# Attention over four head pairs in a row in place of two, with the queries and keys of four pairs kept, in a three-layer kernel on one core

## The chip, the core and the metric

The kernel runs on one NeuronCore of a Trainium2 chip. The metric is the device time of one execution in microseconds (us), the median of several. The engines are TensorE (PE, with its weight loads PEld), VectorE (DVE), ScalarE (ACT), GpSimd (POOL) and SyncE (SP, which here issues DMAs). SBUF is the on-chip memory of 128 partitions, PSUM the accumulators that PE writes. PE, DVE, ACT and POOL each work through their own instructions in program order and wait for each other by semaphores.

## The reference

The input x is 8 batches of 512 rows of 256 numbers, float32. Three residual layers and a fourth that has the third's form:

```
x = x + linear(layernorm(x))     # Q,K,V = xn @ W.T; Q,K normalised by row; Q * mean_n(K * V)
x = x + ffn(layernorm(x))        # r = sigmoid(xr @ W_r.T); k = relu(xk @ W_k.T)**2; r * (k @ W_v.T)
x = x + attention(layernorm(x))  # 16 heads of 64: softmax(q k.T / 8) v, over axis 2; output product l_w, l_b
x = x + ffn(layernorm(x))        # the same weights; xr, xk mix each row with the row before it
```

The softmax of the attention runs over the queries: `scores = einsum('bhqp,bhkp->bhqk', q, k) / sqrt(64)` and `softmax(scores, axis=2)`.

## The kernel before

All weights stay in SBUF. The program is written out without loops on the chip, in an order that a planner in the Python code (`class Order`) chooses while the kernel is built. It knows five engines T (PE), A (ACT), V (DVE), G (POOL), S (SP), an estimated cost for each step, the time at which each engine and each of its five PSUM places comes free, and a due period for every piece of work. `CHOICES` holds three numbers for each period: an offset of the share of other work, a slack, and a seed that reorders pieces that are equally ready.

**Attention.** The 8 batches have 16 heads each, so 8 head pairs a batch and 64 pairs in all, numbered g. For a pair, `scores(g, c)` computes a chunk of 128 keys against 512 queries for both heads in four 64x64 quarters of PE's array; DVE takes the maximum over the queries (L1100) and ACT the exponentials with their sums (L1111). `scale_v(g, h)` divides the values by the sums (DVE reciprocal L1124, POOL L1128). `context(g, c)` multiplies, again in quarters (L1148), into two PSUM places, which ACT and DVE empty at the pair's end (L1155, L1156). Score tiles take three places of two banks each (`PAIRS = 3`), contexts two of one bank (`BANKS = 2`).

`attend(g)` writes two pairs: the first pair's scores alternate with the contexts of the pair before it, the second's with the first's. The main loop goes over `range(0, G, 2)`. After each two pairs comes a stretch of work on the whole 128x128 array: all that the planner has due by then or finds a share for. The stretches of quarter-array and of whole-array work thus alternate, 32 times over.

**Whole-array work.** `project_pairs(g)` makes queries and keys of pairs g and g+1 in seven block products instead of eight (`seven`, L931 for the products; its sums of blocks on ACT and DVE at L939, L947, L883, L893, L903). Product 2 goes into the PSUM place of product 1, 4 into that of 7, 3 into that of 5, and each waits until the place's first content has been read. The results stand in `qk` tiles of the pool `heads`, two buffers. `values_fast` does the same for the values, `keys` for the keys of an ffn (L591), `project_out` the output product (tile `y`, L440) of four pairs, whose `ctx` tiles come from the pool `cpool` with eight buffers.

`linear(b, h)`, `queries`, `mean`, `front` and `ffn` (called f0 to f7 after the linear layer, g0 to g7 after the attention) take half a batch each. From batch 2 on, and for the g ffns but the last, the rows are turned by a DMA transpose (`normed_dma`, SP, between two POOL copies), and both halves' keys are made together by `keys` in seven products from sums of blocks in the tile `sums`. Otherwise `mixed_t` turns them on PE and each half has its own four products for k (L551). Queries, keys and values of a batch need its sums of rows `xts` (`sums_of_rows`, POOL), of which there is one buffer.

Due periods around the change: linear and first ffn of batch b by `due_of`, period 8b-3; `project_pairs(g + 1)` at the end of each period; `values_fast` two or four periods later than its start; `project_out(b, half)` gated to pair 8b+5 or 8b+9.

Of the kernel before, what the change touches and what calls it, by code (L numbers as in the profile page):

```python
# [35 lines left out]


CHOICES = (
    (-4, 2, 90203), (0, 0, 43155), (0, 2, 0), (-2, 2, 77416), (1, 0, 8249), (-2, 1, 93964),
    (0, 0, 0), (-6, 1, 43070), (-2, 0, 51517), (-2, 2, 70093), (-2, 2, 81842), (-1, 2, 0),  # L40
    (1, 0, 13647), (6, 0, 84141), (1, 0, 16079), (4, 1, 90125), (-6, 0, 25271), (0, -1, 56854),
    (-2, 2, 47130), (0, -1, 47424), (0, 1, 8929), (4, 0, 14836), (-6, 0, 64258), (4, 2, 13478),
    (-1, 1, 84848), (2, 2, 74886), (1, 2, 58853), (4, 2, 96692), (6, 0, 82127), (4, 0, 41997),
    (0, 0, 0), (-1, -1, 26368), (6, 0, 83164), (0, 0, 0),
)


# [29 lines left out]
class Order:  # L77
# [5 lines left out]
    def __init__(self):  # L83
        self.free = {"T": 0.0, "A": 0.0, "V": 0.0, "G": 0.0, "S": 0.0}
        self.chains, self.period, self.spent, self.count = [], -1, 0.0, 0
        self.open = -1
        self.marks = {None: 0.0}

        self.banks = [0.0] * (PAIRS + BANKS)
        self.current, self.at = None, 0.0  # L90
# [83 lines left out]

    @property
    def choice(self):
        return CHOICES[min((self.period + 1) // 2, len(CHOICES) - 1)]

    def turn(self, c):

# [47 lines left out]
            self.run(self.first([c for c in a if c not in late] or a))  # L228

    def finish(self):  # L230
        self.period = self.open = 10**6
        while self.chains:
            self.run(self.first(self.able()))
# [3 lines left out]
def kernel(ctx: ExitStack, tc: tile.TileContext, a: dict, out: bass.AP):  # L237
# [18 lines left out]
    two = ctx.enter_context(tc.tile_pool(name="two", bufs=2))  # L256
    small = ctx.enter_context(tc.tile_pool(name="small", bufs=8))
    epool = ctx.enter_context(tc.tile_pool(name="epool", bufs=5))
    cpool = ctx.enter_context(tc.tile_pool(name="cpool", bufs=8))
    heads = ctx.enter_context(tc.tile_pool(name="heads", bufs=2))  # L260
    psum = ctx.enter_context(tc.tile_pool(name="psum", bufs=1, space=bass.MemoryType.PSUM))
    halves_v = ctx.enter_context(tc.tile_pool(name="halves_v", bufs=4))
    ctx.enter_context(tc.manual_schedule())
# [66 lines left out]
    def buffers(own):  # L330

        if own not in sets:
            s = {
                n: one.tile([P, 2, 512], F32, tag=f"{n}{own}", name=f"{n}{own}")
                for n in ("xn", "xr", "xk")
            }

            s["ka"], s["r"] = s["xn"], s["xk"]
            s["sums"] = one.tile([P, 3, HS], F32, tag=f"sums{own}", name=f"sums{own}")
            sets[own] = s  # L340
        return sets[own]

# [19 lines left out]
    def normed(src, name, s, h, ready, early=False):  # L362

        ready = yield "V", 1.2, ready
        mv = small.tile([P, 2, 2], F32, tag="mv", name=f"mv_{name}_{h}")
        for u in range(2):
            st = small.tile([P, 6], F32, tag="st", name=f"st_{name}_{h}_{u}")
            nc.vector.bn_stats(st, src[:, 2 * h + u, :])
            nc.vector.bn_aggr(mv[:, u, :], st)
        xn, rstd = tiles(s["xn"], h), small.tile([P, 2], F32, tag="rstd", name=f"rstd_{name}_{h}")  # L370
        if early:

            ready = yield "G", 1.05, ready
            nc.gpsimd.tensor_scalar(rstd, mv[:, :, 1], LN_EPS, 1.0, ALU.add, ALU.mult)
            nc.gpsimd.tensor_tensor(rstd, rstd, neg_half[:, :2], ALU.pow)
            ready = yield "V", 0.75, ready
            for u in range(2):
                nc.vector.tensor_scalar(
                    xn[:, u, :], src[:, 2 * h + u, :], mv[:, u, 0:1], rstd[:, u : u + 1],
                    ALU.subtract, ALU.mult,  # L380
                )
        else:

            shift = small.tile([P, 2], F32, tag="shift", name=f"shift_{name}_{h}")
            ready = yield "G", 1.4, ready
            nc.gpsimd.tensor_scalar(shift, mv[:, :, 0], -1.0, None, ALU.mult)
            nc.gpsimd.tensor_scalar(rstd, mv[:, :, 1], LN_EPS, 1.0, ALU.add, ALU.mult)
            nc.gpsimd.tensor_tensor(rstd, rstd, neg_half[:, :2], ALU.pow)
            nc.gpsimd.tensor_tensor(shift, shift, rstd, ALU.mult)
            ready = yield "A", 1.0, ready  # L390
            for u in range(2):
                nc.scalar.activation(
                    xn[:, u, :], src[:, 2 * h + u, :], AF.Identity,
                    bias=shift[:, u : u + 1], scale=rstd[:, u : u + 1],
                )
        return ready
# [135 lines left out]
    def ffn(xb, name, s, h, ready, add_on, by_dma, due):  # L532
# [5 lines left out]
        mixed, ready = yield from mix(xb, name, s, h, ready, xr, xk)  # L538
        ka, r = chunks(s["ka"], h), s["r"][:, h, :]
        squared, mark = 0.0, None  # L540
        if by_dma:

            r, mark = s["xr"][:, h, :], (name, "k", h)
            if both((name, "k")):
                order.add(keys(name, s, mixed), *due)
        else:
            done = yield "T", BANK, mixed
            ps = bank(f"k_{name}_{h}")
            for dc in range(KC):
                for kc in range(KC):  # L550
                    nc.tensor.matmul(  # L551
                        ps[:, dc * HS : (dc + 1) * HS], lhsT=fk[:, kc, dc * P : (dc + 1) * P],
                        rhs=xk[:, kc, :], start=(kc == 0), stop=(kc == KC - 1),
                    )
            done = yield "A", 0.6, done
            ps = ps.rearrange("p (k s) -> p k s", k=KC)
            nc.scalar.activation(ka, ps, AF.Relu)
            order.give()
            squared = yield "A", 0.6, done
            nc.scalar.activation(ka, ka, AF.Square)  # L560
# [74 lines left out]
                order.add(linear(b, h), *due_of(b))  # L635

    def due_of(b):
        return (-1 if b == 0 else NP * b - 3), NP

    def adder(b):  # L640

# [9 lines left out]
    def linear(b, h):  # L651
# [16 lines left out]
        for u in range(2):  # L668
# [5 lines left out]
                    start=(kc == 0), stop=(kc == KC - 1),  # L674
                )
            ready = yield "A", 0.8, ready
            vs = two.tile([P, D], F32, tag="av", name=f"av_{b}_{h}_{u}")
            nc.scalar.copy(vs, ps[:, D:])
            nc.scalar.activation(kv[:, u, :], ps[:, :D], AF.Square, accum_out=ss[:, u : u + 1])
            if u == 1:  # L680
                order.add(queries(b, h), *due_of(b))
            ready = yield "V", 0.35, ready
            nc.vector.tensor_mul(kv[:, u, :], ps[:, :D], vs)
            order.give()
        rn = small.tile([P, 2], F32, tag="rn", name=f"rnk_{b}_{h}")
        ready = yield from power(rn, ss, b, h, 0, ready)

# [135 lines left out]
    def sums_of_rows(b, ready):  # L823
# [2 lines left out]
        (b11, b12), (b21, b22) = (  # L826
            (xta[b][:, kc, :HS], xta[b][:, kc, HS:]) for kc in range(KC)
        )
        for i in range(4):
            last = f"qk_{NP * b - 2}" if b else None  # L830
            ready = yield "G", 0.8, ready, -1, last
# [186 lines left out]
    def project_out(b, half):  # L1018
# [1 line left out]
        pairs = range(half * NP // 2, (half + 1) * NP // 2)  # L1020
        lead = 2 * NP * (b == B - 1)
        for tp in range(NT // 2):
            ready = yield "T", 2 * BANK, 0.0, NP * b + 5 + 4 * half
            ps = rows(
                f"y_{b}_{half}_{tp}",
                [ctxt[b, p][:, tp * HS : (tp + 1) * HS] for p in pairs],
                [al[:, p, :] for p in pairs],
            )
            ready = yield "V", 0.62, ready
            xt = half_of(x[b], tp)  # L1030
            nc.vector.tensor_tensor(xt, ps, xt, ALU.add)  # L1031
            order.give()
            if half == 1:
                due = NP * (b + 2) + 1, lead
                order.add(tail(b, tp, ready, due), *due)
        if half == 0:
            order.add(project_out(b, 1), NP * b + 11, lead)
# [120 lines left out]
            ready = order.place("A", 0.5, ready)  # L1158
            order.banks[PAIRS:] = [ready, order.place("V", 0.62, ready)]

    def attend(g):

        for c in range(NT):
            if c == 3:
                order.at_once(scale_v(g, 0))
            scores(g, c)
            if g > 0:
                context(g - 1, c)
            else:
                order.fill(BANK)  # L1170
            exps(g, c)
            order.fill(0.0, 1.0)
        for c in range(NT):
            scores(g + 1, c)
            if c == 1:
                order.at_once(scale_v(g, 1))
            if c > 0:
                context(g, c - 1)
            if c == 3:
                context(g, 3)  # L1180
            exps(g + 1, c)
            order.fill(0.0, 1.0)


    G = B * NP
# [25 lines left out]

    total = B * (2.2 + 6 * BANK + 42 * FAST + 0.43 + 8 * BANK + 2 * FFN) - 4 * BANK - 2 * FFN
    total -= 17 * 1.1 + 7 * 1.1
    total += 2 * FAST - 13 * FAST / 2
    for first in range(0, G, 2):
        g = order.period = first + 1
        order.place("T", CHANGE, 0.0)
        attend(first)
        order.place("T", CHANGE, 0.0)
        order.open = g  # L1220
        for h in range(2):
            order.add(scale_v(g, h), g, 2 * G)
        b, p = divmod(g, NP)
        if p == 5:
            order.add(project_out(b, 0), g + 2)
        if g + 1 < G:
            order.add(project_pairs(g + 1), g, NP)
        if p == 1 and b > 0:
            order.add(values_fast(b, 1), g + 2, NP)
        elif p == 3 and b < B - 1:  # L1230
            order.add(values_fast(b + 1, 0), g + 4, NP)
        share = (total - order.spent) / ((G - first) // 2) + order.choice[0]
        begin = order.spent
        order.until(g, share)
        if g < G - 1:
# [55 lines left out]
```

## Time and profile before

| what | us |
|---|---|
| median of 3 runs | 1146.74 (1146.02 to 1146.79) |
| the profiled execution | 1146.73 |
| its span in the profile | 1144.8 |
| PE busy | 1125.2 |
| DVE busy | 806.0 |
| ACT busy | 679.5 |
| POOL busy | 478.9 |
| first matmul starts at | 6.4 |
| first scores start at | 71.33 |
| last matmul group starts at | 1138.36 |

The page gives busy times, time lines and groups of instructions by line. A line of a time line reads: start, length (both us), engine, line, operation, output and inputs by the program's names, array part in use, shape of the moving operand, and how many instructions were merged. PE takes two passes for each float32 matmul of the program, so the counts of the trace are twice the program's. The ends of matmuls are modelled; their starts are measured. In a row of groups, the numbers behind the bar are busy time and mean length in ns. In a row of windows, the first two numbers bound the stretch, the third is its length, then come the busy times of PE, PEld, DVE, ACT and POOL.

### The profile page before, as it was taken

How to read it: one execution, taken by the hardware profiler on the slowest of the kernel's cores; microseconds unless marked ns; L12 is line 12 of the kernel's file. 1: busy time of each engine (PE TensorE's matmuls, PEld its weight loads, DVE VectorE, ACT ScalarE, POOL GpSimd, SP SyncE). 2: the span in 40 equal slices, each digit the busy share in tenths (PEclk: the TensorE clock that was granted, in tenths of full speed). 3: DMA queues.
4: the chain of work that ended last, by engine and by line, in shares of the span. 5: the costliest groups of instructions: out<-in, count | busy, mean ns of one | idle time of the engine just before them, and what ended most of it. 6: DMA issues, size and time to landing. Idle time of an engine off the chain costs nothing. (4 is left out here: it accounts for less than half of the span.)

```text
span 1144.8 us, 19233 instructions
## 1 busy us (share of the span) xinstructions
PE 1125.2 (98%) x6994; PEld 699.2 (61%) x6994; DVE 806.0 (70%) x1474; ACT 679.5 (59%) x1789; POOL 478.9 (42%) x760
## 2 busy tenths in 40 slices
PE   7999999999999999999999999999999999999998
PEld 4645456656556567666656555766656756665556
DVE  5775777667777767767677777777677777667754
ACT  3546756467663864655655676466574566645653
POOL 4455263224712484217542267343553442523201
PEclk9999999999999999999999999999999999999999
DMA  8000000000001110012100111010200110001001
GB/s 298 1 1 1 1 19 19 10 11 11 19 11 38 29 28 10 10 37 38 20 10 11 37 32 25 10 47 10 29 19 1 22 35 2 19 19 20 1 2 37
DMA packets 61182, 28.64 MB, mean 25 GB/s; under 512 B 51456, under 2 KB 59648, under 8 KB 60576
## 3 DMA queue, kind: packets, MB, share of 16 engines
q1 hardware_dynamic: 59936, 25.70, 9.2%
q8 instruction: 56, 0.92, 0.3%
q10 hardware_dynamic: 864, 1.05, 0.3%
q0 software_dynamic: 288, 0.67, 0.2%
q14 instruction: 38, 0.31, 0.1%
HBM read 10.63 MB, written 4.19 MB: 13 GB/s over the span
## 5 line engine op out<-in xcount | busy, mean ns | idle before, releaser
L1111 ACT ACTIVATE e<-sc,nm 128x512 f32<-128x512 f32 x512 | 347.1, 690 | 123.1 <-DVE nm L1100 123.1
L1100 DVE TENSOR_REDUCE nm<-sc 128x2 f32<-128x1024 f32 x256 | 308.9, 1218 | 69.3 <-PE sc L1095 68.6
L1095 PE MATMUL sc<-qk 64*64 64x512 f32 x2048 | 270.1, 594 | 2.6 <-DVE qk L903 1.7
L1148 PE MATMUL cx<-e,vs 64*64 64x512 f32 x2048 | 269.1, 589 | 0.0
L1128 POOL TENSOR_TENSOR vs<-v,rs 128x256 f32<-128x256 f32 x128 | 79.0, 618 | 381.8 <-DVE rs L1124 353.6
L1148 PEld LDWEIGHTS cx<-e,vs 64*64 64x64 f32 x2048 | 87.2, 133 | 136.9 <-issue 114.5
L1095 PEld LDWEIGHTS sc<-qk 64*64 64x64 f32 x2048 | 76.1, 132 | 138.9 <-issue 86.8
L440 PE MATMUL y<-al,ctx 128*128 128x256 f32 x512 | 116.4, 380 | 0.4 <-ACT prev_f L517 0.4
L440 PEld LDWEIGHTS y<-al,ctx 128*128 128x128 f32 x512 | 96.6, 190 | 17.5 <-ACT e L1111 3.2
L1111 ACT ACTIVATION_READ_ACCUMULATOR e<-sc,nm 128x1 f32 x512 | 105.3, 206 | 0.0
L939 ACT ACTIVATE qk<-m_qk,bias 128x256 f32<-128x256 f32 x124 | 52.2, 475 | 51.7 <-PE m_qk L931 50.1
L1156 DVE TENSOR_TENSOR ctx<-cx,ctx 128x512 f32<-128x512 f32 x64 | 44.3, 692 | 47.3 <-ACT ctx L1155 46.3
L947 DVE SCALAR_TENSOR_TENSOR qk<-m_qk,dbias,qk 128x256 f32<-128x256 f32 x124 | 54.1, 478 | 18.3 <-PE m_qk L931 17.7
L1031 DVE TENSOR_TENSOR x<-y,x 128x512 f32<-128x512 f32 x32 | 22.0, 687 | 35.5 <-PE y L440 35.4
L672 PE MATMUL kv<-wkv,xrl 128*128 128x512 f32 x96 | 44.9, 595 | 0.0
L1155 ACT COPY ctx<-cx 128x512 f32<-128x512 f32 x64 | 37.4, 585 | 10.4 <-PE cx L1148 10.4
L931 PE MATMUL m_qk<-xta,sums_q 128*128 128x256 f32 x124 | 38.0, 388 | 1.0 <-DVE qk L893 0.9
L931 PE MATMUL m_qk<-xta,aq 128*128 128x256 f32 x124 | 38.8, 394 | 0.0
L931 PE MATMUL m_qk<-xts,aq 128*128 128x256 f32 x124 | 37.4, 383 | 0.4 <-DVE qk L883 0.4
L931 PE MATMUL m_qk<-xta,ak 128*128 128x256 f32 x124 | 36.9, 379 | 0.0
L931 PE MATMUL m_qk<-xts,ak 128*128 128x256 f32 x124 | 36.9, 379 | 0.0
L931 PE MATMUL m_qk<-xta,sums_k 128*128 128x256 f32 x124 | 36.9, 379 | 0.0
(303 smaller groups left out, 1941.8 us busy)
## 6 DMA issues: line engine op xcount, KB each, us to landing
out<-x SPq DMA_DIRECT2D x16, 256.0 KB, 2.1
x<-in_x SPq DMA_DIRECT2D x6, 512.0 KB, 4.0
aq<-in_aq SPq DMA_DIRECT2D x1, 1024.0 KB, 8.1
ak<-in_ak SPq DMA_DIRECT2D x1, 1024.0 KB, 10.1
av<-in_av SPq DMA_DIRECT2D x1, 1024.0 KB, 12.1
al<-in_al SPq DMA_DIRECT2D x1, 1024.0 KB, 14.5
x<-in_x ACTq DMA_DIRECT2D x4, 128.0 KB, 4.0
x<-in_x SPq DMA_DIRECT2D x4, 128.0 KB, 4.1
```

The lines of the kernel that those rows point to most:

```text
L440: nc.tensor.matmul(ps[:, u * D : (u + 1) * D], lhsT=lhs[i][:, u * P : (u + 1) * P], rhs=rhs[i], start=(i == 0), stop=(i == n - 1),)
L672: nc.tensor.matmul(ps, lhsT=xt[:, kc, u * P : (u + 1) * P], rhs=wkv[:, kc, :], start=(kc == 0), stop=(kc == KC - 1),)
L931: nc.tensor.matmul(ps[:, w * HS : (w + 1) * HS], lhsT=lhs[w][n - 1], rhs=block_of_rows(b, n), start=start and w == 0, stop=True, skip_grou ...
L939: nc.scalar.activation(dst[:, w, :], ps[:, w, :], AF.Identity, bias=bias[:, w, p : p + 1])
L947: nc.vector.scalar_tensor_tensor(dst[:, w, :], ps[:, w, :], dbias[:, w, p // 2 : p // 2 + 1], part[:, w, :], ALU.add, ALU.add,)
L1095: nc.tensor.matmul(ps[m * HD : (m + 1) * HD, j, :], lhsT=kt[hs, keys], rhs=qt[hs, :], start=True, stop=True,)
L1100: nc.vector.tensor_reduce(nm, ps, AX.X, ALU.max, negate=True)
L1111: nc.scalar.activation(e[:, j, :], ps[:, j, :], AF.Exp, bias=nm[:, j : j + 1], accum_out=sums[g, h][:, c % 2, j : j + 1],)
L1128: nc.gpsimd.tensor_tensor(vs, vh[b, p // 4][:, 2 * h : 2 * h + 2, cols].rearrange("p t (j d) -> p t j d", j=2), rs.unsqueeze(3).to_broadca ...
L1148: nc.tensor.matmul(cx[m][j * HD : (j + 1) * HD, :], lhsT=vsc[g, c // 2][ks, c % 2, j, :], rhs=es[g, c][ks, j, :], start=(c == 0), stop=(c ...
L1155: nc.scalar.copy(ct, cx[0])
L1156: nc.vector.tensor_tensor(ct, cx[1], ct, ALU.add)
```

## The change

- `attend(first, n)` writes n pairs in a row: first two stretches of two pairs, then fifteen of four (`range(4, G, 4)`), so that a batch has two stretches of attention and two of whole-array work.
- `heads` has four buffers for `qk` in place of two; each period projects two times two pairs.
- To make room: `cpool` has seven buffers in place of eight; the first ffn's `sums` tile is gone, so its keys (`name[0] == "f"`) are made in eight plain products, four for each half, as the other path has them; `shift` and `rstd` share a tile; `linear` writes a copy of the values into `xk` in place of a tile of its own.
- `queries(b, h)` are entered after both value products in place of after the first; ACT squares before it copies there.
- `sums_of_rows` waits explicitly for the values of the batch before. Due periods and gates follow the longer period, values are entered after the pairs 3 and 7, and `CHOICES` has 20 rows in place of 34, with other numbers.

```diff
-    cpool = ctx.enter_context(tc.tile_pool(name="cpool", bufs=8))
-    heads = ctx.enter_context(tc.tile_pool(name="heads", bufs=2))
+    cpool = ctx.enter_context(tc.tile_pool(name="cpool", bufs=7))
+    heads = ctx.enter_context(tc.tile_pool(name="heads", bufs=4))
...
-        if by_dma:
+        if by_dma and name[0] == "g":
             r, mark = s["xr"][:, h, :], (name, "k", h)
...
-        return (-1 if b == 0 else NP * b - 3), NP
+        return (-1 if b == 0 else 3 if b == 1 else NP * b - 1), NP
...
-            vs = two.tile([P, D], F32, tag="av", name=f"av_{b}_{h}_{u}")
+            nc.scalar.activation(kv[:, u, :], ps[:, :D], AF.Square, accum_out=ss[:, u : u + 1])
+            vs = tiles(s["xk"], h)[:, u, :]
             nc.scalar.copy(vs, ps[:, D:])
-            nc.scalar.activation(kv[:, u, :], ps[:, :D], AF.Square, accum_out=ss[:, u : u + 1])
-            if u == 1:
-                order.add(queries(b, h), *due_of(b))
...
+        order.add(queries(b, h), *due_of(b))
...
+        if b:
+            yield "G", 0.0, 0.0, -1, f"v_{b - 1}_1"
...
-            ready = yield "T", 2 * BANK, 0.0, NP * b + 5 + 4 * half
+            ready = yield "T", 2 * BANK, 0.0, NP * b + 7 + 4 * half
...
-    def attend(g):
+    def attend(first, n):
         for c in range(NT):
             if c == 3:
-                order.at_once(scale_v(g, 0))
-            scores(g, c)
...
+        for g in range(first + 1, first + n):
+            for c in range(NT):
+                if c == 3 and g < first + n - 1:
+                    order.at_once(scale_v(g, 0))
+                scores(g, c)
+                if c == 1:
+                    order.at_once(scale_v(g - 1, 1))
+                if c > 0:
+                    context(g - 1, c - 1)
+                if c == 3:
+                    context(g - 1, 3)
+                exps(g, c)
+                order.fill()
...
-    for first in range(0, G, 2):
-        g = order.period = first + 1
+    for first, n in [(0, 2), (2, 2)] + [(g, 4) for g in range(4, G, 4)]:
+        g = order.period = first + n - 1
...
-        if g + 1 < G:
-            order.add(project_pairs(g + 1), g, NP)
-        if p == 1 and b > 0:
-            order.add(values_fast(b, 1), g + 2, NP)
-        elif p == 3 and b < B - 1:
-            order.add(values_fast(b + 1, 0), g + 4, NP)
+        for i in range(g + 1, min(g + (3 if g == 1 else 5), G), 2):
+            order.add(project_pairs(i), g, NP)
+        if p == 3 and b > 0:
+            order.add(values_fast(b, 1), g, NP)
+        if p == 7 and b < B - 1:
+            order.add(values_fast(b + 1, 0), g, NP)
```

## The prediction

> **What bounds the kernel now.** I read the page's busy times first, then TensorE's waits, then the time line across two changes of array mode, then the windows of single stretches. The page:
>
> ```profile
> span 1144.8 us, 19233 instructions
> PE 1125.2 (98%) x6994; PEld 699.2 (61%) x6994; DVE 806.0 (70%) x1474; ACT 679.5 (59%) x1789; POOL 478.9 (42%) x760
> PEclk9999999999999999999999999999999999999999
> ```
>
> TensorE (PE) works from 6.4 us until 4.6 us before the end, at the full granted clock. No other engine is above 70%, so the time is PE's work plus the moments in which PE cannot go on. The waits that the profile lists are few:
>
> ```profile
> engine line waited for: us in total, times, longest us
> PE tr_a L406 <- DVE xnFalse L378: 6.4, 1, 6.4
> PE sc L1095 <- DVE qk L903: 1.7, 4, 0.4
> PE m_qk L931 <- DVE qk L893: 0.9, 2, 0.4
> ```
>
> But matmul ends are modelled, so short stops hide in a busy PE. Starts show them. Sixteen passes of y take 3.45 us, so a 128x256 pass steps by 0.216 and a 64x512 pass in a group of eight by 0.107. The time line around one whole-array stretch (lines left out between the third and the fourth):
>
> ```profile
> 303.41 1.90 PE L1148 MATMUL cx<-e,vs 64*64 64x512 f32 x16
> 305.24 0.70 PE L931 MATMUL m_qk<-xta,aq 128*128 128x256 f32 x2
> 305.77 0.59 PE L931 MATMUL m_qk<-xta,ak 128*128 128x256 f32 x2
> ...
> 322.32 0.70 PE L591 MATMUL m_k_g<-xkTrue,sums_f 128*128 128x256 f32 x2
> 322.95 1.09 PE L1095 MATMUL sc<-qk 64*64 64x512 f32 x8
> 323.86 1.04 PE L1148 MATMUL cx<-e,vs 64*64 64x512 f32 x8
> ```
>
> Into the whole array: 16 x 0.107 = 1.72 should end at 305.13, the next starts at 305.24 and its pair takes 0.53 for 0.43, so 0.20 lost. Back into quarters: 0.63 for 0.43 includes a wait's 0.10, and 0.91 for 0.86, so 0.15 lost. A round trip costs 0.35 us. The same bookkeeping over all passes of the run: 4096 x 0.1074 + 2658 x 0.2156 + 176 x 0.431 + 64 x 0.108 = 1095.8 us of work; 37 quarter-array stretches x 0.35 = 13.0; 6.4 before and 4.6 behind; the remaining 25 us are short waits. 8.0 of them lie before the first scores at 71.3, 1.7 in the tail, some 15.3 between, about 12.5 in whole-array stretches and 2.8 in quarter ones. One of the dearest:
>
> ```profile
> 476.09 0.59 PE L591 MATMUL m_k_g<-sumsTrue,sums_f 128*128 128x256 f32 x2
> 477.11 0.70 PE L931 MATMUL m_qk<-xts,aq 128*128 128x256 f32 x2 [0.42 <-DVE qk L883]
> ```
>
> 1.02 for 0.43: 0.59 of waiting and 0.10 in the next pass, where product 7 follows its predecessor's DVE add too closely. A wait just missed costs 0.18 in the same way (0.08 and 0.10).
>
> **Part by part.** The sum is made on the profiled execution: 1146.73 us, of which 1144.8 is the span and 1.9 lies around it; the median of the runs, 1146.74, is the same.
>
> *Round trips.* In the order of the changed program's PE instructions I count 23 quarter-array stretches for 37. They are the 17 of the loop, the last pair's contexts, one break in the first attention (before: 32, 1 and four) and four cuts in three later ones, after a first chunk of scores: there a PSUM place that attention needs is still held by products that must be finished first. 14 x 0.35 = -4.9.
>
> *Keys of the first ffn.* Batches 2 to 7 take eight products per batch for seven. The rows for m_k_f count 24 + 24 + 24 + 12 passes over six batches, 14 a batch, so a product is two passes, 0.43 us. 6 x 0.43 = +2.6, on the path, since PE is. What leaves with it is beside the path: four POOL subtractions of 0.73, five DVE adds of 0.42, two ACT copies of 0.38 a batch. PE's work is thus -2.3.
>
> *The opening.* Before, four whole-array blocks (v, r_f, o_f, k_f of batch 1) stand between the first scores and fill PE while exponentials run; 71.3 to 122 is nearly without waits. In the new order only one (v, 0.86) is left; the others come earlier. I walk it with the trace's durations (scores 0.86, reduction 1.16, pair of exponentials 1.33, three score banks): fourth scores wait for the first exponentials, the eighth start at 11.0 us, the stretch ends at 13.6. Its work is 12 x 0.86 + 0.86 + 0.7 of changes = 11.9, so +1.7. Next stand the 14 matmuls of project_pairs(2) alone, 6.0 us, with nothing between the dependent products: begin on ACT behind the last exponentials at 15.7, add 17.3, join 18.2, product 4, add, product 3 from 19.2 to 20.1, last add, scores at 21.0. That is 7.4 us for 6.0, so +1.4. Together +3.1; bounds 0 (a cover I overlooked) and 5.
>
> *Tail.* The last matmul is now o_g of batch 6, whose sum goes to POOL (1.27) where before o_g of batch 7 went to DVE (0.69): +0.6. Bounds 0 and 2.
>
> *Waits between.* Neither edit names these; the new order decides them. I compared, in both orders, each waiting matmul's cover (PE work since the product that its chain starts from) with the chain (the rows' durations). Beyond the opening 32 waits of before have a chain longer than the cover, 41 of after. The dearest new one: r_g(4,0) stands 1.72 us behind o_f(6,1), while its input needs that bank's DVE release (0.68), four ACT passes (1.9) and a DVE pair (0.88): 1.6 us. Two contexts at starts of stretches (pairs 15 and 47) wait for a last add of keys, 0.6 each; scores of pair 60 for 0.7. By such sums after has some 2 us more. Against that, stretch ends, where a last product, its add and the first scores stand in a row, come half as often. I take +1.3; bounds -6 (the in-between waits shrink by 40%, with the stretches) and +8 (each of the nine further waits at 0.9).
>
> *Longer quarter stretches.* From the third pair on, a pair finds what the second found before: exponentials of the pair ahead end 9.0 us after that pair's start in both places of the trace. The windows of one stretch of two pairs:
>
> ```profile
> core 0: us, PE busy (x) PEld busy (x) DVE busy (x) ACT busy (x) POOL busy (x), PEclk, DMA share, GB/s
> 322.90:336.80 13.90, 13.90 (x129) 4.77 (x128) 11.64 (x15) 10.24 (x29) 1.23 (x2) 1.00 0.00 1
> ```
>
> DVE is at 84% and ACT at 74% while PE is full, and 28 of 32 stretches show no wait at all, so four pairs cost 0. [...]
>
> *At nothing.* The av tile now lies in xk: same ACT and DVE instructions, square before copy. Queries enter one product later, covered by a stretch of 30 us and more. ctx has seven buffers: the first y of a batch must run in the stretch before the eighth ctx, and does. POOL's wait of the row sums for the values of the batch before has only the chain's later steps behind it, at 42% load; SP issues the same transposes and stores, with DMA at 10%. Were that cover gone, a late transpose would show its 3.0 us to landing once a batch.
>
> Sum: -4.9 + 2.6 + 3.1 + 0.6 + 1.3 = +2.7, **1149.4 us**.
>
> **Rivals.** *Waits go with the number of stretches* (faster). If the 15.3 us between the opening and the tail belong to starts and ends of stretches, halving these takes 7.6: -4.9 + 2.6 + 3.1 + 0.6 - 7.6 = -6.2, 1140.5; it beats no change from 3.2 us of saved waits (21% of them). For it: the chains of two pairs cover each other's adds. Against: about half of the 32 tight waits stand at such an end, but the count of 41 for the new order has its fewer ends in it already. *Opening covered* (about the same): without 3.1 and with waits unchanged, -1.7, 1145.0; without the latter's third, within 0.2%. *Banks* (much slower): two product chains hold up to six of five banks, next to ffn and values; in the order, product 7 of both pairs often waits for the other's add. If each of the 15 stretches pays one wait like the 0.69 at 477.11 on top, +10, 1159. Against: DVE has 12.6 us less to do.
>
> **How the numbers follow.** About 0.2% (2.3 us) is what a measurement here can tell from no change. Forecast case, 1147.5 to 1152: 0.45. Fewer waits, 1139 to 1144.5: 0.25. Covered opening, 1144 to 1147.5: 0.15. Banks, 1152 to 1160: 0.15. Of the forecast case 0.10 lies below 1149.0, of the covered one 0.03 below 1144.4. Faster 0.28, same 0.22, slower 0.50. The range leaves out the ends of the first and last rivals: 1142 to 1156, of which 1147.5 to 1152 is the likeliest case's own.
>
> **What would show it.** The 84 passes of m_k_f gone and 96 of k_f in their place, 2.6 us more; the quarter stretches 27.5 us long without waits inside; a stop of over 1 us before r_g of batch 4's first half; a first stretch of 13 to 14 us, followed by 7 us of m_qk alone. If starts of PE lose less than 20 us beyond the round trips, I am wrong towards the fast side; if the 27.5 us stretches show a wait at each new pair, my reading of the steady state is wrong; if DVE waits before product 7 add up to 5 us or more, the banks have it.

## The result, and the profile after

The changed kernel takes **1171.81 us** (median of 4 runs, 1169.46 to 1172.51), the kernel before, beside it on the same chip, 1146.62 (1146.02 to 1146.79). The ratio is 1.0214, 95% interval [1.0202, 1.0227]: 25 us slower. The forecast said 1149.4 with a range up to 1156; the direction was right, the size was not.

The page of the changed kernel, the lines that answer to those of before (the profiled execution took 1172.51 us):

```profile
span 1170.7 us, 19410 instructions
PE 1132.7 (97%) x7006; PEld 709.3 (61%) x7006; DVE 790.1 (67%) x1444; ACT 677.7 (58%) x1777; POOL 462.9 (40%) x736
PEclk9999999999999999999999999999998999999999
```

DVE and POOL have less to do than before, as the plain keys promise, and PE is still the engine that sets the time. PE's granted clock, 9 in every slice before, now shows one 8. What PE waits for, from the view of waits (us in total, times, longest):

```profile
PE r_g L441 <- DVE xrTrue L524: 3.9, 3, 1.9
PE sc L1097 <- DVE qk L905: 2.9, 3, 1.6
PE kv L673 <- POOL xrl L429: 2.7, 1, 2.7
...
PE k_f L552 <- issue: 1.2, 1, 1.2
PE m_k_g L592 <- DVE xnTrue L895: 1.2, 1, 1.2
PE m_qk L933 <- DVE qk L885: 1.1, 1, 1.1
```

Before, no wait after the first matmul was listed at over 0.9 us; here there are stops of 1.9 and 2.7 us. The same bookkeeping over the starts of PE's passes as in the prediction gives this table. "Waits" is the span less the first matmul's start, the work, 0.35 us for each quarter-array stretch, and the tail; it holds the opening's waits and the passes at half clock too. All columns behind the median are of the profiled execution. The last six rows are of experiments told below.

| kernel | median, us | span | work of PE | stretches: round trips | waits |
|---|---|---|---|---|---|
| before | 1146.62 | 1144.8 | 1095.8 | 37: 13.0 | 25.1 |
| after | 1171.81 | 1170.7 | 1098.4 | 23: 8.0 | 52.7 |
| before, other table (e3) | 1151.32 | 1149.5 | 1095.8 | 37: 13.0 | 29.8 |
| after, other table (e4) | 1165.32 | 1165.0 | 1098.4 | 22: 7.7 | 47.4 |
| after, SP counted, other table (e9) | 1150.09 | 1148.6 | 1098.4 | 23: 8.0 | 30.5 |
| the same with eight places (e10) | 1140.13 | 1138.1 | 1098.4 | 22: 7.7 | 20.8 |
| before, both, other table (e14) | 1134.97 | 1132.6 | 1095.8 | 37: 13.0 | 12.9 |
| after, both, other table (e15) | 1136.70 | 1134.9 | 1098.4 | 24: 8.4 | 17.4 |

So the whole miss is in one column: waits went from 25.1 to 52.7 us, +27.6, where the forecast had +1.3 and +3.1 for the opening. Most of it sits in few places. Three whole-array stretches, in the view of windows (bounds, length, busy PE, PEld, DVE, ACT, POOL, clock):

```profile
285.60:334.10 48.50, 45.48 (x192) 34.61 (x188) 33.40 (x73) 22.09 (x59) 32.71 (x51) 1.00 0.11 21
706.60:761.20 54.60, 51.59 (x219) 40.75 (x215) 31.73 (x72) 25.78 (x66) 32.25 (x51) 0.97 0.12 25
845.60:910.80 65.20, 59.50 (x244) 46.23 (x240) 38.79 (x93) 33.73 (x82) 45.02 (x69) 0.95 0.13 25
```

By their passes they hold 43.55, 49.16 and 54.76 us of work: 4.9, 5.4 and 10.4 us are lost, 20.8 of the 52.7 (1.6 and 2.7 of it, in the last two, at half clock, told at the end). No engine is full in them: DVE is at 58 to 69%, ACT at 46 to 52%, POOL at 59 to 69%. And yet PE waits for each of them in turn. The time line ahead of the dearest stop, cut to POOL, SP's queue and the waiting product:

```profile
714.33 1.17 POOL L420 COPY xrl<-xnl 128x512 uint16<-128x512 uint16 x2
715.70 1.31 SPq L425 DMA_TRANSPOSE xnl<-xrl  x1
717.74 1.34 POOL L429 COPY xta<-xkFalse 128x1024 uint16<-128x1024 uint16 x1 [0.60 <-DMA xkFalse<-xrFalse]
719.01 1.27 POOL L784 TENSOR_TENSOR x<-x,lb 128x512 f32<-128x512 f32 x1
720.22 1.33 POOL L429 COPY xrl<-xnl 128x1024 uint16<-128x1024 uint16 x1
721.60 0.70 PE L673 MATMUL kv<-wkv,xrl 128*128 128x512 f32 x1 [2.65 <-POOL xrl L429]
```

Transposes land 3.1 us after issue (median of this run), so `xrl`'s data were there at about 718.8. The copy that turns them into an input for PE starts at 720.22, because the addition of an output bias, for which nobody waits, stands in front of it in POOL's list. One of the three stops before `r_g`, cut to PE, ACT and DVE:

```profile
871.07 1.89 PE L441 MATMUL o_f<-fv,xnFalse 128*128 128x256 f32 x8
871.27 0.60 ACT L565 ACTIVATE xkFalse<-r_f 128x512 f32<-128x512 f32 x1 [1.23 <-PE r_f L441]
871.76 0.98 ACT L518 ACTIVATE prev_g<-xrTrue,omu 128x255 f32<-128x255 f32 x2
...
873.07 0.69 DVE L570 SCALAR_TENSOR_TENSOR xkFalse<-xkFalse,o_f 128x512 f32<-128x512 f32 x1 [1.23 <-PE o_f L441]
873.88 0.87 DVE L524 SCALAR_TENSOR_TENSOR xrTrue<-xrTrue,mu,prev_g 128x256 f32<-128x256 f32 x2
874.50 1.97 PE L441 MATMUL r_g<-fr,xrTrue 128*128 128x256 f32 x8 [1.55 <-DVE xrTrue L524]
```

`r_g` is a product of the last ffn of batch 4, `r_f` and `o_f` belong to the first ffn of batch 6: no data pass between them. But ACT's shifted rows for `r_g` stand behind ACT's tanh of `r_f`, which waits for PE; and DVE's mix for `r_g` stands behind DVE's product with `o_f`, which waits for PE as well. Two chains that have nothing to do with each other are tied together by the order of the lists, and PE, whose own list is in order too, waits at each knot.

### The profile page after: what moved, and what is told of

Read it like the earlier page. It is cut to its first block, busy times and chain, and to the rows that moved or that the text cites. A ratio compares the mean times of both kernels' runs of the same rounds, so it can differ in the third digit from the quotient of the medians.

```text
span 1170.7 us, 19410 instructions
## 1 busy us (share of the span) xinstructions
PE 1132.7 (97%) x7006; PEld 709.3 (61%) x7006; DVE 790.1 (67%) x1444; ACT 677.7 (58%) x1777; POOL 462.9 (40%) x736
## 5 line engine op out<-in xcount | busy, mean ns | idle before, releaser
L1097 PE MATMUL sc<-qk 64*64 64x512 f32 x2048 | 267.2, 592 | 4.3 <-DVE qk L905 2.9
L1150 PEld LDWEIGHTS cx<-e,vs 64*64 64x64 f32 x2048 | 90.4, 133 | 137.8 <-issue 107.8
```

Of the source, the lines that this page charges most:

```text
L1097: nc.tensor.matmul(ps[m * HD : (m + 1) * HD, j, :], lhsT=kt[hs, keys], rhs=qt[hs, :], start=True, stop=True,)
L1150: nc.tensor.matmul(cx[m][j * HD : (j + 1) * HD, :], lhsT=vsc[g, c // 2][ks, c % 2, j, :], rhs=es[g, c][ks, j, :], start=(c == 0), stop=(c ...
```

## The experiments

Theories, from the expectations: **structure** (two long whole-array stretches a batch leave chains uncovered in whatever order), **order** (the loss lies in the particular order), **chain** (data arrive late along norm, sum and transpose), **queues** (in e5 to e7: ACT, DVE and POOL are too full in the long stretches; from e8 on: a step stands behind steps of other chains in its engine's list), **banks** (too few PSUM places), **eight products**.

### Two kernels with flat tables (e1, e2)

```diff
-CHOICES = (
...
-)
+CHOICES = (
+    (0, 0, 0),
+)
```

> The kernel before, with its table of choices flat: every row (0, 0, 0), so that neither shares, slack nor tie-breaks are bent; the same work in another order. It says how much of 1146.7 us the table carries. Theory 'structure' (two long whole-array stretches a batch leave the chain of steps of a batch uncovered, in whatever order): the table is worth little, 1150 to 1165. Theory 'order' (the loss of 25 us lies in the particular order that the changed kernel's table gives, not in the length of the stretches): a table carries more than the whole difference, over 1172 here.

> The changed kernel with the table flat in the same way. Structure: 25 us above the flat kernel before, give or take 5, since the stretches are what costs. Order: also tens of us above 1172; its distance to the flat kernel before may be anything between -20 and +40, because each is one draw of an order. A distance near +25 alone would not tell the two apart; the next two runs do.

Measured, one run each: 1223.59 and 1235.18. The table carries 77 us in the kernel before and 63 in the changed one, two and a half to three times the difference that was to be explained. "Structure" had expected 1150 to 1165 for the first. The distance of 11.6 is one draw of each and tells nothing alone.

### Tables drawn alike (e3, e4)

The rows of `CHOICES` alone are others.

> The kernel before with a table drawn anew: rows chosen one after the other, with a fixed number of tries each, for the least idle TensorE that the kernel's own planner foresees. It is the yardstick for the next run, same procedure. Both theories: 1146 to 1156, as the table of before is a good one already.

> The changed kernel with a table drawn anew in the same way; everything else as in the changed kernel (four pairs a period, eight products, buffers). Structure: 1163 to 1172, within 9 us of the changed kernel, and some 20 us above the run before it. Order: 1146 to 1158, that is 14 to 26 us below the changed kernel, and within 8 us of the run before it; the stops of over 1 us in whole-array stretches, some 20 us in the changed kernel, fall to less than 8.

Measured: 1151.32 (ratio to before 1.0039 [1.0025, 1.0053]) and 1165.32 (1.0162 [1.0135, 1.0189]). Both theories had the first run. The second is 6.5 us below the changed kernel and 14.0 above its yardstick: inside what "structure" had (1163 to 1172, within 9 us of the changed kernel), though it had put some 20 us above the yardstick, and outside what "order" had (1146 to 1158). So after this pair "structure" stood the better. But the trace of the second shows where its worst stop comes from, and it is a queue that nobody had counted:

```profile
660.78 0.38 SPq L1054 DMA_DIRECT2D out<-x  x1
662.96 0.38 SPq L273 DMA_DIRECT2D x<-in_x  x1
663.44 1.24 SPq L425 DMA_TRANSPOSE xkTrue<-xrTrue  x1
668.47 1.32 POOL L429 COPY xrTrue<-xkTrue 128x1024 uint16<-128x1024 uint16 x1 [6.43 <-DMA xkTrue<-xrTrue]
669.82 0.19 ACT L512 COPY edge_g<-xrTrue 128x2 f32<-128x2 f32 x1 [6.05 <-POOL xrTrue L429]
669.92 0.98 ACT L518 ACTIVATE prev_f<-xrFalse,omu 128x255 f32<-128x255 f32 x2
670.83 0.82 ACT L941 ACTIVATE qk<-m_qk,bias 128x256 f32<-128x256 f32 x2
671.71 0.70 PE L933 MATMUL m_qk<-xta,sums_q 128*128 128x256 f32 x2 [4.27 <-ACT qk L941]
```

The store of a finished batch (L1054) and the load of a new one into the same tile (L273, which waits for the store) stand on SP ahead of a transpose; the transpose, 3.9 us after the POOL copies that feed it ended at 659.52, then takes 4.9 us behind the 512 KB of the load in place of 3.1. POOL waits for it, ACT's two-number copy of an edge waits for POOL, and behind that copy stand the activations that PE needs. The planner gave the store and the load no time on SP.

### The data cut, the order kept (e5, e6)

```diff
     def normed(src, name, s, h, ready, early=False):
+        if name[0] == "g" or name[1:] not in ("0", "1"):
+            src = al
         ready = yield "V", 1.2, ready
```

> The changed kernel, every instruction in the same order, but the norms of batches 2 to 7 and of all last ffns read the rows of a weight that is long there, in place of the batch's rows. So no norm waits any more for a sum that TensorE's products feed; the steps behind a norm, the queues, the PSUM places and the work stay as they are (the output is that of other rows). Theory 'chain' (products wait for the steps that run from one product over a sum, a norm, POOL's copies, a transposing DMA to the next product, and with two stretches a batch too little else stands between): the waits outside the opening fall by more than half, 1140 to 1153. Theory 'queues' (ACT, DVE and POOL, in order, are too full in the long whole-array stretches, whoever feeds them): 1162 to 1172. Theory 'banks' (too few PSUM places): 1162 to 1172 as well, with the waits behind adds of products left.

> The same cut in the kernel before, order kept. Chain: it has little to gain, as an attention stretch of 14 us lies over each link: 1138 to 1146, a gain of less than a third of that of the changed kernel. Queues and banks: 1144 to 1148, no gain.

Measured: 1172.13 (1.0214 [1.0197, 1.0231]) and 1146.71 (0.9995 [0.9986, 1.0004]). Nothing moves. The stops are at the same products with the same lengths (2.77, 1.71 and 2.38 us where the changed kernel has 2.82, 1.71 and 2.10, by the starts of passes). "Chain" in the form in which I held it is refuted: that a norm waits for its rows costs nothing in these orders. What a norm's later steps wait for, their data or their turn, this run does not tell.

### One kind of POOL step taken out (e7)

```diff
-        nc.gpsimd.tensor_tensor(xh, xh, lb.to_broadcast([P, 2, D]), ALU.add)
```

> The changed kernel without the 16 POOL additions of the output bias (1.32 us each, left out of the result), all else in the same order. In the changed kernel's trace one of them stands between two POOL copies of which the second is what TensorE waits for longest (2.65 us at 721.6). Chain: this stop falls by 1.3 us, others hardly, 1166 to 1171. Queues: POOL has 21 us less to do, of which a good part is in the whole-array stretches: 1155 to 1165. Banks: no change, 1169 to 1173.

Measured: 1168.58 (1.0183 [1.0168, 1.0198]), 3.2 us less. The stop at `kv` goes from 2.82 to 1.51 us, that is by the 1.3 us of the addition in front; the three stops from 871 on stay (1.71, 2.12, 2.36). The half-clock passes behind the `kv` stop (told at the end) are gone too (mean granted clock 0.999 for 0.995), and a stop of 1.4 us before the next `r_g` has come in. The time is in the range of "chain", which e5 had already refuted; "queues" in its form of too full engines had 1155 to 1165 and fails. Of some 20 us of POOL work (16 additions of 1.27) leaving it out gained 3.2, part of it clock: here the position of a step counted, not the load.

### Shifted rows in SBUF (e8)

```diff
-            ps = bank(f"prev_{name}_{h}_{i}").rearrange("p (k s) -> p k s", k=KC)
+            order.take()
+            ps = two.tile([P, 512], F32, tag="prev", name=f"prev_{name}_{h}_{i}")
+            ps = ps.rearrange("p (k s) -> p k s", k=KC)
...
```

> The changed kernel, order kept; the shifted rows of a time mix ('prev', two ACT passes and two DVE steps each) lie in SBUF instead of one of PSUM's five places (their two buffers take the room of the value bias, for which another weight's row is read). Theory 'banks' (products and prevs queue for five places): the waits of ACT for a place, and TensorE's behind them (the stops of 1.5 and 1.9 us before r_g at 874 and 878), fall: 1150 to 1164. Theory 'queues' (each engine works its list in order, so that a step stands behind a step of another chain that itself waits for TensorE): within 4 us of the changed kernel, 1168 to 1173.

Measured: 1178.03 (1.0270 [1.0253, 1.0287]), 6 us slower: inconclusive for the question, since the edit changed something else. DVE's mixing steps, here (L525) and in the changed kernel (L524), duration ns min/median/max:

```profile
L525 DVE SCALAR_TENSOR_TENSOR xkTrue<-xrTrue,mu,prev_g x28: 472/486/1487, 298.9 to 1135.3; 128x256 f32<-128x256 f32 x28
L525 DVE SCALAR_TENSOR_TENSOR xrTrue<-xrTrue,mu,prev_g x28: 472/798/1504, 305.4 to 1139.2; 128x256 f32<-128x256 f32 x28
```

```profile
L524 DVE SCALAR_TENSOR_TENSOR xkTrue<-xrTrue,mu,prev_g x28: 472/478/482, 298.7 to 1129.3; 128x256 f32<-128x256 f32 x28
L524 DVE SCALAR_TENSOR_TENSOR xrTrue<-xrTrue,mu,prev_g x28: 473/478/481, 305.0 to 1132.7; 128x256 f32<-128x256 f32 x28
```

With one operand in PSUM all these steps take 472 to 482 ns; with both in SBUF up to three times that.

### The order, with SP counted (e9), and eight places (e10)

```diff
+        stored = yield "S", 0.4, order.marks["g", b, h]
         nc.sync.dma_start(out=rows_out[:, ts, :], in_=x[b][:, ts, :])
         if both(f"g{b}") and b + 4 < B:
+            yield "S", 2.4, stored
             load_x(b + 4)
...
+        if b == 0:
+            ready = max(ready, order.marks.get("sums_q", 0.0), order.marks.get("sums_k", 0.0))
         order.marks["xts", b] = ready
```

> The changed kernel with another order: its planner also counts the store of a finished batch and the load of a new one on SyncE's queue (they were free for it, and in the run with the table drawn anew two transposes behind such a load landed after 6.0 and 4.9 us in place of 3.1, with stops of 3.5 and 4.3 us behind them), and the table is drawn anew and longer. Same periods, eight products, buffers and places. Theory 'order' (the loss lies in how the steps are put in order): 1145 to 1156, with no stop over 2 us after the first scores. Theory 'structure' (two stretches a batch cost it in any order): above 1160, like the table drawn before (1165.3).

Measured: **1150.09** (1.0025 [1.0014, 1.0035]), 21.7 us below the changed kernel with the same periods, the same products, buffers and places; only the order differs. That it lies 0.7 from the forecast is luck: it is another order than the one that was forecast. "Structure" is refuted at this size. One part of the expectation failed: three stops of 2 us and more are left (by starts of passes 3.6 before scores, 2.5 before an `r_g`, 2.0 before an `o_g`). Three things were done together: SP's store and load are counted, batch 0's products are planned behind the sums of the weights (the last lines shown; in e4 PE had waited 2.5 us at 102.5 for POOL's `sums_k`), and the table was searched for longer. The run does not divide the 15.2 us from e4 between them.

For eight places, PSUM becomes one tile cut by hand, and the second halves of the score places may be taken in whole-array stretches:

```diff
+    places = psum.tile([P, 2 * PAIRS + BANKS, 512], F32, tag="ps", name="places")
     def psum_tile(i, name):
-        shape = [P, 2, 512] if i < PAIRS else [P, 512]
-        return psum.tile(shape, F32, tag=f"ps{i}", name=name)
+        if i < PAIRS:
+            return places[:, 2 * i : 2 * i + 2, :]
+        if i < PAIRS + BANKS:
+            return places[:, PAIRS + i, :]
+        return places[:, 2 * (i - PAIRS - BANKS) + 1, :]
...
-        self.banks = [0.0] * (PAIRS + BANKS)
+        self.banks = [0.0] * (2 * PAIRS + BANKS)
...
```

> As the run before it, and in whole-array stretches the second halves of the three score places serve as places of their own: eight in place of five. One PSUM tile, cut by hand; table drawn anew with this. Banks: 6 to 15 us below the run before it, 1135 to 1148. Without an effect of places: within 5 us of it. If the hand-cut tile adds waits of its own between places, above it.

Measured: **1140.13** (0.9937 [0.9922, 0.9952]): 10 us below e9, as "banks" had it, and 7 below the kernel before. The table is another one too; e12 and e13 keep the order.

### Only the eight products (e11)

```diff
-        if by_dma:
+        if by_dma and name[0] == "g":
```

> The kernel before (two pairs a period, four stretches a batch) with only one part of the change: the first ffn's keys in eight products; table drawn anew, with less effort than its own had. TensorE has 2.6 us more work, POOL 17.5 us less. Theory 'eight products' (what follows from the plain keys costs the 25 us): over 1162. All others: 1147 to 1157.

Measured: 1162.14 (1.0132 [1.0117, 1.0147]), just over the border that "eight products" had set (over 1162). By starts of passes PE's work is the expected +2.6 us; 37 us are waits, one of 4.9 us before a context. As the table changes with the edit, the run alone does not acquit the products; e9, e10 and e15, with eight products in each, do.

### Eight places without a new order (e12, e13)

```diff
+    turns = [0] * PAIRS
+    def other_half(i, ps):
+        if i >= PAIRS:
+            return ps
+        turns[i] = 1 - turns[i]
+        return ps[:, turns[i], :]
...
-        return ps[:, 0, :] if i < PAIRS else ps
+        return other_half(i, ps)
...
```

> The changed kernel, same order, same five places; only PSUM is one tile cut by hand instead of five tiles. A control for the next run: 1169 to 1174 if the hand-cut tile changes no wait.

> The control's kernel, same order on every engine, but successive products (and shifted rows) that the plan puts into the same score place alternate between its two halves, so that a product no longer waits for the emptying of the one before it in that place. Eight places for whole-array work without any change of order. Theory 'banks': a good part of the 25 us are waits for a place: 1150 to 1165. Theory 'queues in order': the places are free, but the instruction that a product waits for still stands behind others in its engine's list: 1167 to 1172, less than 5 us gained. Then what eight places brought before (10 us against 1150.1) came through the order that they allow.

Measured: 1171.47 (1.0214 [1.0199, 1.0229]) and 1168.50 (1.0187 [1.0170, 1.0204]). The hand-cut tile costs nothing, and places alone give 3 us, about half of it clock: the executions of e12 at a granted clock of 0.999 and 1.0 took 1170.14 and 1169.63, those of e13 at 0.999 took 1167.98 to 1168.72. "Banks" is refuted as the cause of the 25, "queues" in its second form has it as expected. The stops stay where they were (in e13 2.84, 1.71, 2.17, 2.28 us). So the 10 us of e10 came with its new table: from orders that more places allow, or from the luck of the draw, which moved e15 by another 3.4; the runs do not part the two.

### Both kernels treated alike (e14, e15)

e14 is the kernel before with the edits of e9 and e10; e15 is e10 with its table drawn on.

> The kernel before (two pairs a period, seven products) with what made the changed kernel fast: store and load counted on SyncE's queue, eight places in whole-array stretches, a table drawn anew with the same effort as in the next run. If the longer periods are worth their -4.9 us of round trips, the next run is faster than this one by 2 to 8 us; if the loss of 25 us was theirs in part ('structure'), this one is faster by over 8; if periods hardly matter beside the order, the two lie within 5 us. This one: 1133 to 1142.

> The changed kernel with eight places as measured before at 1140.1, its table drawn on with the same effort as that of the run above: 1136 to 1141.

The table of e14:

```
CHOICES = (
    (-1, 2, 60400), (-2, -1, 0), (0, -1, 55218), (-1, 2, 91593), (0, 0, 18972), (-6, 0, 22473),
    (0, 0, 59382), (0, 2, 63756), (4, 1, 70041), (1, 2, 0), (-4, 0, 96360), (1, -1, 0),
    (0, 1, 0), (6, 0, 98383), (2, 0, 0), (1, 0, 0), (1, 1, 99514), (6, 1, 2300),
    (-2, 0, 68612), (0, -1, 40918), (1, 2, 58732), (-4, 1, 0), (4, -1, 91028), (1, 1, 10137),
    (4, -1, 85044), (-4, 0, 88403), (2, 1, 8031), (1, 0, 0), (4, 1, 0), (-1, -1, 6304),
    (4, 2, 67402), (0, -1, 49043), (-4, 0, 0), (-2, 2, 41408),
)
```

Measured: **1134.97** (0.9896 [0.9882, 0.9911]) and 1136.70 (0.9912 [0.9897, 0.9926]). Both beat both kernels; e14 is the fastest seen. Its page, and the waits of over 1 us that e15 has left beyond the opening:

```profile
span 1132.6 us, 19130 instructions
PE 1116.7 (99%) x6994; PEld 705.7 (62%) x6994; DVE 806.2 (71%) x1474; ACT 679.3 (60%) x1789; POOL 479.4 (42%) x760
```

```profile
PE places L447 <- DVE xrTrue L530: 2.1, 1, 2.1
PE places L558 <- ACT places L524: 1.1, 1, 1.1
```

The two lie 1.7 us apart, inside the 5 that were expected if periods hardly matter beside the order, and less than one more round of search moved the changed kernel (3.4, from e10 to e15). In the table above the terms are: round trips -4.6, work +2.6, waits +4.5, to the disfavour of the longer periods. In these two orders the longer periods give back in waits what they save in changes of mode, and the change as such is worth about nothing.

## Why the prediction was wrong, and where it was right

- **Round trips, right.** 23 quarter-array stretches for 37, and a clean long one of four pairs shows the price:

```profile
195.66:223.30 27.64, 27.64 (x257) 9.73 (x256) 22.38 (x29) 22.40 (x63) 5.00 (x10) 1.00 0.01 1
```

27.64 us for 256 x 0.1074 = 27.49 of work: 0.15 lost, as before; the other 0.20 of a round trip falls into the stretch behind.
- **Longer quarter stretches, right.** DVE at 22.38 and ACT at 22.40 of 27.64 us (81%) keep up, with no wait at the start of a new pair. Five of the fifteen stretches lost 0.6 to 2.0 us more, singly.
- **Eight products, right**: PE's work +2.6. **Opening, right in its parts**: the first stretch took 14.4 us for 12.7 of work and changes, 1.6 lost (forecast 1.7; its 13.6 for 11.9 counted `v` at 0.86, which is 1.72 of work), and the 14 matmuls of two pairs alone took 7.6 (forecast 7.4 with 6.0 of work). The waits before the first scores, which the sum left as they were, fell from 8.0 to 6.7. **Tail, right**: 5.14 for 4.59, +0.55 (forecast +0.6).
- **The named stop** before `r_g` of batch 4's first half is there, 1.94 us for 1.6. But its neighbours, 1.55 before `r_g` of the other half and 1.2 before `k_f`, were not in the list.
- **The step that failed is "Waits between"**: +1.3 with bounds of -6 and +8, where +27.6 came, some 24 with the opening's 3 taken off. I compared each product's cover with the length of its own chain, as if a chain's steps began when their inputs are there. In these orders they begin when their turn comes. The trace of before had shown this nowhere at length, since it was an order with few such knots; my count of 32 tight waits against 41 therefore measured the data, whose lateness at the norms costs nothing (e5), and not the lists: another order of the same work takes 21.7 us less (e9). How much of the 24 each knot holds is shown for the stop before `kv` alone (1.3 us, e7); for the others it is read from the time lines. The upper bound of +8 priced nine further waits and no longer ones at the places already counted.
- **Banks** fails by its own sign: DVE waits before product 7 come to 1.9 us (1.1 and 0.8), under the 5 that I had named. **Fewer waits** fails outright; its border was off besides, as with -4.9 + 2.6 + 3.1 + 0.6 = +1.4 it breaks even from 1.4 us of saved waits and is clear of no change from 3.7, not 3.2.
- Said of the opposing case and worth keeping: half the stretch ends did not halve the waits, neither in the shipped order (52.7) nor in the best (17.4 against 12.9).

Open: why this change came with an order this bad. Tables drawn the same way left the changed kernel 14.0 us behind with five places (e3, e4) and 1.7 with eight (e14, e15), so the longer periods seem harder to order when places are few; that is an inference from one table each, and not shown.

## What to carry to other kernels

Where engines work through lists in order, the wait that a new order brings is not read from data chains: walk each engine's list across the stretch, and ask of every step in front of the one that PE needs what that step itself waits for, SP's stores and loads among them. A change that comes with a new hand-tuned order is judged by giving both sides an order found in the same way; here, with eight places on both sides too, that turned a loss of 25 us into one of 2. And a stretch in which no engine is full can still lose 10 us, if all the work left in it hangs on chains that are knotted by position.

## What the hardware showed beside it

**Half clock behind a stop.** After the 2.82 us stop at 721.6 PE's passes take twice their time (a 128x256 pass steps by 0.43 us for 0.216), and so again after the row of stops from 874 on. The view of windows (clock in the column before the last two) for the changed kernel, then for e12, which has the same order and stops of 2.77, 1.71, 2.17 and 2.27 us at the same products, and then for e9, where a stop of 2.54 us ended at 991.34; in the last two the clock stayed:

```profile
721.80:725.40 3.60, 3.60 (x6) 1.71 (x6) 3.49 (x11) 0.89 (x3) 2.05 (x3) 0.55 0.09 18
879.30:885.90 6.60, 5.43 (x13) 3.85 (x13) 2.71 (x10) 4.08 (x9) 5.55 (x7) 0.50 0.21 40
```

```profile
720.50:724.10 3.60, 3.60 (x12) 2.18 (x13) 3.49 (x10) 1.10 (x3) 2.22 (x3) 1.00 0.04 8
877.10:884.00 6.90, 4.61 (x18) 3.06 (x18) 2.17 (x8) 4.54 (x11) 5.80 (x9) 1.00 0.23 45
```

```profile
988.50:991.50 3.00, 0.62 (x4) 0.25 (x3) 0.95 (x3) 1.65 (x4) 2.84 (x6) 1.00 0.61 98
991.50:994.50 3.00, 3.00 (x14) 2.44 (x14) 0.30 (x2) 0.86 (x2) 2.92 (x4) 1.00 0.41 80
```

That is 3.6 x 0.45 = 1.6 us and 5.43 x 0.50 = 2.7 us of the loss in the profiled execution of the changed kernel; with flat tables the mean granted clock fell to 0.984 (e1) and 0.976 (e2). In the changed kernel the view of windows has a granted clock of 1.00 for 718.00:722.17, 0.50 for 722.17:725.58 and 1.00 again for 725.60:730.00; then 1.00 for 874.00:879.17, 0.50 for 879.18:886.00 and 1.00 for 886.05:890.00. So the passes were slow for 3.4 us the first time and for 6.8 us the second. The first time followed a stop of 2.82 us, the second two in a row of 1.71 and 2.10, while nearly the same stops in e12 changed nothing. So the length of a stop alone does not decide it; what does, no run here shows.

**DVE and POOL.** Mixing steps of DVE with both tensors in SBUF took 472 to 1507 ns in e8. At 873.16 us two of them took 2.81 us while POOL ran two additions of 128x512 (873.03 to 875.69); at 868.42 two took 0.88 while the POOL step beside them was one of 128x2. Whether POOL's additions are what makes them long, no run here tests. In the changed kernel, with the shifted rows in PSUM, all 104 of these steps took 472 to 482 ns.
